# Attention and quantised feed-forward on one core: the softmax weights turned by VectorE and DMAs over DRAM, one place later

## The chip, the cores and the metric

One core of a Trainium2 chip runs the whole program. The metric is device time in microseconds (us): the median of the runs, 797.94 us before the change. TensorE does matrix products and turns matrices, VectorE and ScalarE work elementwise and on rows, GpSimd (POOL in the profile) takes elementwise work that needs no PSUM, and SyncE (SP) issues the DMAs.

## The reference

16 sequences of 256 tokens, 256 features. Attention has 16 query heads and 4 key/value heads of 128; a query sees itself and the 31 tokens before it (the window), and the first 4 tokens (the sink). The feed-forward part is a product with rows and weights rounded to 8 bits.

```python
# x: (16, 256, 256); layernorm without gain
x = x + attn(layernorm(x))
x = x + ffn(layernorm(x))

# attn: q = x @ wq.T (16 heads of 128), k, v = x @ wk.T, x @ wv.T (4 heads, each shared by 4 query heads)
mask = (k <= q) & ((k < 4) | (k >= q - 31))
scores = q . k / sqrt(128)
ex = exp(where(mask, scores, lowest) - rowmax) * mask
out = (ex / max(sum(ex), 1e-9)) @ v ;  return out @ wo.T

# ffn: per row of x and of weight: scale = max|.| / 127, rounded to int8
y = (x_q @ w_q.T) * x_scale * w_scale + bias
```

## The kernel before

**Tiles.** Activations are kept transposed. A *unit* (n, g, t) is one sequence, one key/value head g with its 4 query heads, and one half t of the tokens; 16 x 4 x 2 = 128 units. A unit has four blocks of 32 queries; with 4 heads these are 128 rows, which meet only 68 keys: the 4 sink keys, the 32 of the block before, and their own 32. So the scores of a unit are four products of 128x128 by 128x68 (`pss`, L503). A float32 product is two passes on TensorE, a transpose one.

**One unit's way.** VectorE scales and masks the scores out of PSUM (L514) and takes the row maximum (L516); ScalarE takes four exponentials with their sums (L523); VectorE divides (L530 to L533). Then the weights, 128 queries x 68 keys, must have keys on the partitions: TensorE turns each block (`ptd`, L508), and ScalarE copies the result to SBUF (`ad`, L511). With the values `vw`, laid out as 68 rows per block, four products give `po` (L539), which ScalarE copies to `oT` (L551). The output weights give `py` (L578, L594).

**The order** is written out by hand, one iteration i per unit, and each engine keeps it (`in_written_order`, L21). In iteration i TensorE runs: the scores of unit i with the transposes of unit i-1 between them (L496 to L508); a part of `py` for an earlier unit; `po` of unit i-1; a *chunk* in some iterations, that is the seven products for the keys or values of two heads of the next sequence (L444, L454); then the seven products for two query heads (`pq`, L470) that are used later. Keys, values, queries and most of `py` use a seven-product (Strassen-Winograd) scheme; the sums that put its results together (`combine`, L281 to L297) run on VectorE for the queries, at the start of the next iteration after L516, and on GpSimd for the chunks. The sums on the attention output before `py` (`left_sums`, L246 to L249) run on GpSimd.

For a fast output, part 0 of `py` (12 passes) comes in iteration i+2 and part 1 (16 passes) in i+3, where unit i is the second half of a head. So even iterations have 16 passes, and odd ones have 12 passes and a chunk: chunks stand in slots -5 (values of heads 0, 1), -3 (keys 0, 1), -1 (keys 2, 3) and +1 (values 2, 3), counted from the first unit of their sequence (L738).

**PSUM banks around the chunk.** The queries have two banks, q0 and q1. A chunk takes one bank of the pool `ps_m` and one of these two, the one that holds the first four results of the `pq` before it (`banks_of_chunk`, L276). The combine operations L293 and L294 read that bank; L295 to L297 read the other.

**Keys and values.** When GpSimd has combined a key chunk into `ktmp`, the keys are copied into 68 columns per block (`keys_to`, L382): two large copies by VectorE (L387, L388), two of 64 columns by ScalarE (L389, L390). This happens 1 iteration after the chunk for heads 0, 1 and 2 after it for heads 2, 3 (`keys_late`). Values go from SBUF to SBUF by 11 DMAs per pair of heads (`values_to`, L392).

**The rest of VectorE's work** stands at the ends of certain iterations: the combine of `py` and the addition to x (L602), the statistics, the norm (`norm`, L624 to L627, with L182), the rounding (L630) and the output (L654) of the feed-forward part in consecutive iterations from slot `done`+1 on (L768), and the norm of a later sequence (L182).

Of the kernel before, what the change touches and what calls it, by code (L numbers as in the profile page):

```python
# [34 lines left out]
def kernel(  # L35
# [27 lines left out]
    SB = T // QB  # L63
    NK = SINK + 2 * QB
    assert WIN == QB and HG * QB == P
    SCALE = 1.0 / math.sqrt(D)
# [4 lines left out]
    p2 = ctx.enter_context(tc.tile_pool(name="p2", bufs=2))  # L71
    p3 = ctx.enter_context(tc.tile_pool(name="p3", bufs=3))
    ps_s = ctx.enter_context(tc.tile_pool(name="ps_s", bufs=1, space=bass.MemoryType.PSUM))
    ps_t = ctx.enter_context(tc.tile_pool(name="ps_t", bufs=1, space=bass.MemoryType.PSUM))
# [28 lines left out]
    wo_sb = const.tile([P, H, DM], FP, name="wo_sb")  # L103
    wf_sb = p1.tile([P, NC, DM], FP, name="wf_sb")
    bias_bc = const.tile([P, DM], FP, name="bias_bc")
# [28 lines left out]
    def keep(ap, base, cm, step):  # L134
# [4 lines left out]
        )  # L139

    def mask_steps():


        def build(b):
            pool.memset(masks[:, 0, b, :], 0.0)
            if b < 2:
                pool.memset(masks[:, 0, b, 0:SINK], NEG)
            if b == 0:
                pool.memset(masks[:, 0, b, SINK : SINK + QB], NEG)
            for h in range(HG):  # L150
                m = masks[h * QB : (h + 1) * QB, 0, b, :]
                keep(m[:, SINK:], QB, 1, -1)
                if b == 1:
                    keep(m[:, 2 * SINK :], SINK - 1, -1, 1)
                elif b == 2:
                    keep(m[:, SINK:], -1, -1, 1)

        def others():
            like = masks[:, 0, 2:3, :]
            pool.tensor_copy(masks[:, 0, 3:, :], like)  # L160
            pool.tensor_copy(masks[:, 1], like.to_broadcast([P, NBLK, NK]))
            pool.tensor_copy(ident16, ident)
            pool.memset(ones, 1.0)

        return [lambda b=b: build(b) for b in (2, 0, 1)] + [others]
# [22 lines left out]
    def ffn_weight_steps():  # L188
        ws = p1.tile([P, NC], FP, name="ws")
        wq16 = p1.tile([P, NC, DM], BF, name="wq16")  # L190
        diag = p1.tile([P, NC, P], FP, name="diag")

# [189 lines left out]
    def keys_to(n, g, kb):  # L382

        k = p2.tile([P, 2, SB, NK], FP, tag="kt", name=f"kt_{n}_{g}")
        for e in range(2):
            kt[n, g + e] = k[:, e]
        dve.tensor_copy(k[:, :, :, SINK + QB :], kb)  # L387
        dve.tensor_copy(k[:, :, 1:, SINK : SINK + QB], kb[:, :, 0 : SB - 1, :])  # L388
        act.copy(k[:, :, 0, SINK : SINK + QB], kb[:, :, 0, :])  # L389
        act.copy(k[:, :, :, 0:SINK], kb[:, :, 0, 0:SINK].unsqueeze(2).to_broadcast([P, 2, SB, SINK]))  # L390

    def values_to(w, v, tiles):  # L392

        if 0 in tiles:
            sp.dma_start(w[0:SINK], v[0:SINK, 0].unsqueeze(1).to_broadcast([SINK, SB, 2 * D]))
            sp.dma_start(w[SINK : SINK + QB, 0, :], v[0:QB, 0])
            sp.dma_start(w[SINK : SINK + QB, NBLK, :], v[P - QB : P, 0])
        for t in tiles:
            sp.dma_start(w[SINK + QB : NK, t * NBLK, :], v[0:QB, t])
            for k in range(1, NBLK):  # L400
                sp.dma_start(w[SINK:NK, t * NBLK + k, :], v[(k - 1) * QB : (k + 1) * QB, t])

# [10 lines left out]
    def plain_values(n, t):  # L413
        pv = ps_m.tile([P, G * D], FP, tag="m", name=f"pv_{n}_{t}")
        for c in range(NC):
            pe.matmul(  # L416
                pv, xnT[n][:, c, t * P : (t + 1) * P], wv_sb[:, c, :],
                start=(c == 0), stop=(c == NC - 1),
            )

        def rest():
            v = p2.tile([P, 3, 2, D], FP, tag="vt", name=f"vt_{n}_{t}")
            act.copy(v[:, 0:2].rearrange("p j e d -> p (j e d)"), pv)
            for p in range(2):
                if t == 0:
                    vw[n, p] = p3.tile([NK, SB, 2 * D], FP, tag="vw", name=f"vw_{n}_{p}")
                plain_values_to(vw[n, p], v[:, p].rearrange("p e d -> p (e d)"), t)

        return rest

    def plain_values_to(w, v, t):
        if t == 0:
            sp.dma_start(w[0:SINK], v[0:SINK].unsqueeze(1).to_broadcast([SINK, SB, 2 * D]))
            sp.dma_start(w[SINK : SINK + QB, 0, :], v[0:QB])
            sp.dma_start(w[SINK : SINK + QB, NBLK, :], v[P - QB : P])
        sp.dma_start(w[SINK + QB : NK, t * NBLK, :], v[0:QB])
        for k in range(1, NBLK):
            sp.dma_start(w[SINK:NK, t * NBLK + k, :], v[(k - 1) * QB : (k + 1) * QB])

# [11 lines left out]
    def values(n, pair):  # L451
        p = banks_of_chunk(f"pv_{n}_{pair}")
        for to, left, right in products(p, factors(n, wv_sb, wv_sums, pair), SMALL_FIRST):
            pe.matmul(to, right, left, start=True, stop=True)  # L454
        v = p2.tile([P, 3, 2, D], FP, tag="vt", name=f"vt_{n}_{pair}")
        w = vw[n, pair] = p3.tile([NK, SB, 2 * D], FP, tag="vw", name=f"vw_{n}_{pair}")
        return Products(p, f"v_{n}_{pair}", (v[:, 0:3:2, 0], v[:, 2, 1], v[:, 1, 0], v[:, 0:2, 1])), (
            lambda: values_to(w, v.rearrange("p j e d -> p j (e d)"), range(NT))
        )

# [31 lines left out]
    def scores_and_turned(u, w):  # L492
# [5 lines left out]
        if w:  # L498
            sw = ss.pop(w)
            ptd = ps_t.tile([NK, NBLK * P], FP, tag="t", name=f"ptd_{w[0]}_{w[1]}_{w[2]}")  # L500
        for k in range(NBLK):
# [5 lines left out]
            if w:  # L507
                pe.transpose(ptd[:, k * P : (k + 1) * P], sw[:, k, :], ident)  # L508
        if w:
            ad = ads[w] = p2.tile([NK, NBLK * P], FP, tag="ad", name=f"ad_{w[0]}_{w[1]}_{w[2]}")  # L510
            act.copy(ad, ptd)  # L511
        if u:
            s = ss[u] = p3.tile([P, NBLK, NK], FP, tag="sc", name=f"s_{n}_{g}_{t}")
            dve.scalar_tensor_tensor(s, pss, SCALE, masks[:, t], ALU.mult, ALU.add)  # L514
            nmax = p3.tile([P, NBLK], FP, tag="nmax", name=f"nmax_{n}_{g}_{t}")
            dve.tensor_reduce(nmax, s, AX.X, ALU.max, negate=True)  # L516
        return nmax if u else None

    def exponentials(n, g, t, nmax):
        s = ss[n, g, t]  # L520
        sm = p3.tile([P, NBLK], FP, tag="sm", name=f"sm_{n}_{g}_{t}")
        for k in range(NBLK):
            act.activation(  # L523
                s[:, k, :], s[:, k, :], AF.Exp, bias=nmax[:, k : k + 1], scale=1.0,
                accum_out=sm[:, k : k + 1],
# [3 lines left out]
    def normalised(n, g, t, sm):  # L529
        dve.tensor_tensor(sm, sm, floor, ALU.max)  # L530
        dve.reciprocal(sm, sm)
        s = ss[n, g, t]
        dve.tensor_mul(s, s, sm.unsqueeze(2).to_broadcast([P, NBLK, NK]))  # L533

    def times_values(n, g, t):
        ad = ads.pop((n, g, t))
        po = ps_m.tile([P, NBLK, HG, QB], FP, tag="m", name=f"po_{n}_{g}_{t}")
        for k in range(NBLK):
            pe.matmul(  # L539
                po[:, k].rearrange("p h i -> p (h i)"), vw[n, g // 2][:, t * NBLK + k, g % 2 * D : (g % 2 + 1) * D],  # L540
                ad[:, k * P : (k + 1) * P], start=True, stop=True,
            )
# [172 lines left out]


    units = [(n, g, t) for n in range(B) for g in range(G) for t in range(NT)]
    units[-3], units[-2] = units[-2], units[-3]
    PER = G * NT

    LAST = ((3, 3), (4, 5), (5, 5), (6, 6), (6, 7), (7, 7), (8, 8), (9, 9))

# [5 lines left out]
    for n in range(B):  # L728
# [8 lines left out]
        else:  # L737
            for slot, f, pair in ((-5, values, 0), (-3, keys, 0), (-1, keys, 1), (1, values, 1)):  # L738
                at(n * PER + slot, lambda f=f, n=n, pair=pair: f(n, pair), chunks)
# [8 lines left out]
    for i, (n, g, t) in enumerate(units):  # L748
        if n == 0:
            at(i + 3, lambda u=(n, g, t): projected(*u), shares)  # L750
        elif n == B - 1:
# [3 lines left out]
        elif t == 1:  # L755
            for part in range(2):
                at(i + 2 + part, lambda u=(n, g, part): projected_fast(*u), shares)
    at(0, lambda: weight_sums(wv_sb, wv_sums))
# [8 lines left out]
    for n in range(B - 1):  # L767
        done = (n + 1) * PER + 2  # L768
        for k, slot in enumerate((1, 2, 3, 4, 5)):
# [24 lines left out]

    waiting, later = None, {}
    for i in range(len(units) + 2):
        u, w = get(i), get(i - 1)
        chunk = chunks.pop(i, [None])[0]
        nmax = scores_and_turned(u, w)
        if waiting:  # L800
            waiting.first()
# [12 lines left out]
        if not shared or i >= (B - 1) * PER:  # L814
            rests += [queries(n, h) for n, h in asked.get(i, []) if not fast_queries(n, h)]
            asked[i] = [u for u in asked.get(i, []) if fast_queries(*u)]
        values_out = times_values(*w) if w else None
        if chunk:
# [4 lines left out]
        if u:  # L823
            normalised(*u, sm)
        if w:
            values_out()
        for f in later.pop(i, []):
# [7 lines left out]
        if chunk:  # L835
# [3 lines left out]
            else:  # L839
                chunk_rest()  # L840
        for f in combined:
# [45 lines left out]
```

## Time and profile before

| what | us |
|---|---|
| median of three runs | 797.94 (797.91 to 798.2) |
| the profiled execution: its own time | 797.91 |
| its span in the profile | 796.1 |
| granted TensorE clock over the span | 0.997 |
| one steady sequence, 8 units (400.47 to 448.82) | 48.35 |
| of it busy: TensorE / VectorE / ScalarE / GpSimd | 48.35 / 37.17 / 26.84 / 32.30 |
| DMA engines busy in that stretch | 0.15 |

A group line of the profile names the line, the engine, the operation, output<-input, the shape and the count; then busy us and mean ns of one; then the idle time of the engine just before, with what ended it. A matmul's record runs until its results are in PSUM and overlaps its neighbours, so the pace of TensorE is read from starts, not from durations. PEld is the load of the stationary operand, which runs ahead under other products. In the timeline the columns are start, time, engine, line, and how many records are merged. TensorE is busy 50.00 of every 50 us until 775 us; the tail from there to 796 is the last feed-forward part.

### The profile page before, as it was taken

How to read it: one execution, taken by the hardware profiler on the slowest of the kernel's cores; microseconds unless marked ns; L12 is line 12 of the kernel's file. 1: busy time of each engine (PE TensorE's matmuls, PEld its weight loads, DVE VectorE, ACT ScalarE, POOL GpSimd, SP SyncE). 2: the span in 40 equal slices, each digit the busy share in tenths (PEclk: the TensorE clock that was granted, in tenths of full speed). 3: DMA queues.
4: the chain of work that ended last, by engine and by line, in shares of the span. 5: the costliest groups of instructions: out<-in, count | busy, mean ns of one | idle time of the engine just before them, and what ended most of it. 6: DMA issues, size and time to landing. Idle time of an engine off the chain costs nothing.

```text
span 796.1 us, 19508 instructions
## 1 busy us (share of the span) xinstructions
PE 787.0 (99%) x7019; PEld 776.2 (97%) x7019; DVE 588.7 (74%) x1716; ACT 433.4 (54%) x1617; POOL 514.3 (65%) x813
## 2 busy tenths in 40 slices
PE   9999999999999999999999999999999999999996
PEld 7999999999999999999999999999999999999994
DVE  3577787787777877877877877877778778778675
ACT  3655555555555555555555555555555555555552
POOL 4768866676676675676666766766766756766423
PEclk9999999999999999999999999999999999999998
DMA  6510201111020110201202011110202102011001
GB/s 217 164 29 14 58 21 48 31 36 49 23 60 17 54 40 15 71 21 42 37 23 63 21 48 31 36 49 22 60 18 56 36 14 71 21 30 36 22 22 33
DMA packets 43808, 35.09 MB, mean 44 GB/s; under 512 B 14144, under 2 KB 42176, under 8 KB 43712
## 3 DMA queue, kind: packets, MB, share of 16 engines
q1 hardware_dynamic: 43712, 33.84, 16.6%
q8 instruction: 56, 0.92, 0.5%
q14 instruction: 40, 0.33, 0.1%
HBM read 9.83 MB, written 4.19 MB: 18 GB/s over the span
## 4 chain that ended last, share of the span: by engine, by line
PE 99%; DVE 1%; issue 0%; POOL 0%; ACT 0%; DVEq 0%; POOLq 0%
PE pq L470 23%; PE py L594 22%; PE po L539 14%; PE pss L503 11%; PE ptd L508 7%; PE pk L444 6%; PE pv L454 6%; PE py L578 3%; PE pq L481 2%; PE pa L649 1%; PE xt L361 1%; PE warm L779 0%; PE pv L416 0%; PE pk L407 0%; PE xt L379 0%; DVE y_last L706 0%
## 5 line engine op out<-in xcount | busy, mean ns | idle before, releaser
L511 ACT COPY ad<-ptd 68x512 f32<-68x512 f32 x128 | 74.4, 581 | 227.8 <-PE ptd L508 227.8
L523 ACT ACTIVATE s<-s,nmax 128x68 f32<-128x68 f32 x512 | 173.6, 340 | 17.4 <-DVE nmax L516 11.0
L503 PE MATMUL pss<-kt,qt 128*128 128x68 f32 x1024 | 151.6, 250 | 0.0
L503 PEld LDWEIGHTS pss<-kt,qt 128*128 128x128 f32 x1024 | 147.4, 191 | 0.7 <-issue 0.5
L508 PE MATMUL ptd<-ident,s 128*68 128x128 f32 x512 | 139.1, 273 | 0.0
L539 PE MATMUL po<-ad,vw 68*128 68x128 f32 x1024 | 135.3, 275 | 0.0
L514 DVE SCALAR_TENSOR_TENSOR s<-pss,masks 128x272 f32<-128x272 f32 x128 | 56.3, 440 | 96.7 <-PE pss L503 92.7
L539 PEld LDWEIGHTS po<-ad,vw 68*128 68x128 f32 x1024 | 125.8, 192 | 1.0 <-ACT ad L511 0.3
L470 PE MATMUL pq<-xs,wq_sums 128*128 128x128 f32 x714 | 118.6, 275 | 0.0
L470 PEld LDWEIGHTS pq<-xs,wq_sums 128*128 128x128 f32 x714 | 98.8, 192 | 0.0
L523 ACT ACTIVATION_READ_ACCUMULATOR s<-s,nmax 128x1 f32 x512 | 95.6, 187 | 0.0
L551 ACT COPY oT<-po 128x512 f32<-128x512 f32 x129 | 75.4, 585 | 30.0 <-PE po L539 30.0
L508 PEld LDWEIGHTS ptd<-ident,s 128*68 128x68 f32 x512 | 84.7, 165 | 0.1
L594 PE MATMUL py<-wo_sums,os 128*128 128x128 f32 x672 | 84.2, 275 | 0.0
L594 PEld LDWEIGHTS py<-wo_sums,os 128*128 128x128 f32 x672 | 79.4, 192 | 0.0
L293 POOL TENSOR_TENSOR ktmp<-b_k 128x256 f32<-128x256 f32 x30 | 21.9, 728 | 86.1 <-ACT b_k L314 86.1
L293 POOL TENSOR_TENSOR vt<-b_v 128x256 f32<-128x256 f32 x30 | 21.8, 728 | 81.2 <-ACT b_v L314 81.2
L246 POOL TENSOR_TENSOR os<-oT 128x256 f32<-128x256 f32 x56 | 46.8, 836 | 40.7 <-ACT oT L551 39.5
L470 PE MATMUL pq<-xnT,wq_sb 128*128 128x128 f32 x476 | 72.6, 275 | 0.0
L470 PEld LDWEIGHTS pq<-xnT,wq_sb 128*128 128x128 f32 x476 | 62.7, 192 | 0.0
L533 DVE TENSOR_TENSOR s<-s,sm 128x272 f32<-128x272 f32 x128 | 58.9, 460 | 4.4
L594 PE MATMUL py<-wo_sb,oT 128*128 128x128 f32 x448 | 59.2, 275 | 0.0
(181 smaller groups left out, 1824.8 us busy)
## 6 DMA issues: line engine op xcount, KB each, us to landing
vw<-vt SPq DMA_DIRECT2D x192, 64.0 KB
vw<-vt SPq DMA_DIRECT2D x160, 32.0 KB
x<-in_x_dram SPq DMA_DIRECT2D x15, 256.0 KB
out_dram<-y SPq DMA_DIRECT2D x15, 256.0 KB
wq_sb<-in_wqT_dram SPq DMA_DIRECT2D x4, 512.0 KB
wo_sb<-in_woT_dram SPq DMA_DIRECT2D x4, 512.0 KB
wv_sb<-in_wvT_dram SPq DMA_DIRECT2D x1, 512.0 KB
wk_sb<-in_wkT_dram SPq DMA_DIRECT2D x1, 512.0 KB
```

The lines of the kernel that those rows point to most:

```text
L444: pe.matmul(to, left, right, start=True, stop=True)
L454: pe.matmul(to, right, left, start=True, stop=True)
L470: pe.matmul(to, left, right, start=True, stop=True)
L503: pe.matmul(pss[:, k, :], qt[n, g][:, t, k].rearrange("p h i -> p (h i)"), kt[n, g][:, t * NBLK + k, :], start=True, stop=True,)
L508: pe.transpose(ptd[:, k * P : (k + 1) * P], sw[:, k, :], ident)
L511: act.copy(ad, ptd)
L514: dve.scalar_tensor_tensor(s, pss, SCALE, masks[:, t], ALU.mult, ALU.add)
L523: act.activation(s[:, k, :], s[:, k, :], AF.Exp, bias=nmax[:, k : k + 1], scale=1.0, accum_out=sm[:, k : k + 1],)
L533: dve.tensor_mul(s, s, sm.unsqueeze(2).to_broadcast([P, NBLK, NK]))
L539: pe.matmul(po[:, k].rearrange("p h i -> p (h i)"), vw[n, g // 2][:, t * NBLK + k, g % 2 * D : (g % 2 + 1) * D], ad[:, k * P : (k + 1) * P ...
L551: act.copy(o[:, t, hs].rearrange("p h (k i) -> p k h i", i=QB), po[:, :, hs])
L594: pe.matmul(region(py, i), left[:, e], right[:, e], start=(g == 0 and e == 0 and i in (1, 4)), stop=(g == G - 1 and e == 1 and i in (7, 3)),)
```

## The change

Units 4 to 122 no longer have their weights turned by TensorE (`lag` 2). VectorE divides in place, in one of two score buffers of 96 columns per block whose last 28 are cleared once, and turns it in 32x32 blocks into `z`. SP stores `z` to DRAM (`zd`), and, in the next iteration, after that has landed, loads it back as `ad`, with 96 rows of keys: row 3j+c is key j of chunk c (0 the block before, 1 its own, 2 the sink). `po` of such a unit comes two iterations after its scores instead of one. The first four and the last five units keep TensorE's transpose, now of 96 columns.

With that the parts of `py` move one iteration later and the chunks to slots -4, -2, 0 and +2 (for sequence 1: -1, -3, 0, +2), so that chunks stand in even iterations, still beside 12 passes. The feed-forward steps move one iteration later. All four key copies are ScalarE's now. Values go to DRAM in one store and come back to three standing buffers by three loads (four the first time each buffer is used), issued one iteration after the chunk.

```diff
+    scores = [const.tile([P, NBLK, NKP], FP, name=f"scores_{j}") for j in range(2)]
+    for j in range(2):
+        pool.memset(scores[j], 0.0)
...
-        dve.tensor_copy(k[:, :, :, SINK + QB :], kb)
-        dve.tensor_copy(k[:, :, 1:, SINK : SINK + QB], kb[:, :, 0 : SB - 1, :])
-        act.copy(k[:, :, 0, SINK : SINK + QB], kb[:, :, 0, :])
-        act.copy(k[:, :, :, 0:SINK], kb[:, :, 0, 0:SINK].unsqueeze(2).to_broadcast([P, 2, SB, SINK]))
+        act.copy(k[:, :, :, QB : 2 * QB], kb)
+        act.copy(k[:, :, 1:, 0:QB], kb[:, :, 0 : SB - 1, :])
+        act.copy(k[:, :, 0, 0:QB], kb[:, :, 0, :])
+        act.copy(k[:, :, :, 2 * QB :], kb[:, :, 0, 0:SINK].unsqueeze(2).to_broadcast([P, 2, SB, SINK]))
...
+    def values_to(n, pair, v, tiles=range(NT)):
+        w, fresh = vw[n, pair], 2 * n + pair < 3
+        b0, b1 = tiles[0] * NBLK, (tiles[-1] + 1) * NBLK
+        sp.dma_start(w[1:NKP:NCH, b0:b1], v[b0:b1].rearrange("b k d -> k b d"))
+        c1 = min(b1 + 1, SB)
+        sp.dma_start(w[0:NKP:NCH, b0 + 1 : c1], v[b0 : c1 - 1].rearrange("b k d -> k b d"))
+        if b0 == 0:
+            rows = QB if fresh else SINK
+            sp.dma_start(w[2 : NCH * (rows - 1) + 3 : NCH], v[0, 0:rows].unsqueeze(1).to_broadcast([rows, SB, 2 * D]))
...
+    def weights_turned(n, g, t):
+        s = ss.pop((n, g, t))
+        z = p2.tile([P, NCH, NBLK, QB], FP, tag="z", name=f"z_{n}_{g}_{t}")
+        dve.transpose(z, s.rearrange("p k (c i) -> p c k i", c=NCH))
+        zd = dram.tile([P, NCH * P], FP, tag="zd", name=f"zd_{n}_{g}_{t}")
+        sp.dma_start(zd, z.rearrange("p c k i -> p (c k i)"))
+        def back():
+            ad = ads[n, g, t] = p3.tile([NKP, HG, NBLK, QB], FP, tag="ad", name=f"ad_{n}_{g}_{t}")
+            sp.dma_start(
+                ad.rearrange("p h k i -> p h (k i)"), zd.rearrange("(h j) (c x) -> (j c) h x", h=HG, c=NCH)
+            )
+        return back
...
-            for slot, f, pair in ((-5, values, 0), (-3, keys, 0), (-1, keys, 1), (1, values, 1)):
+            for slot, f, pair in zip((-4, -2, 0, 2) if n > 1 else (-1, -3, 0, 2), (values, keys, keys, values), (0, 0, 1, 1)):
...
+    FIRST, TAIL = 4, len(units) - 5
+    def lag(i):
+        return 2 if FIRST <= i < TAIL else 1
...
-                at(i + 2 + part, lambda u=(n, g, part): projected_fast(*u), shares)
+                at(i + 3 + part, lambda u=(n, g, part): projected_fast(*u), shares)
...
-        done = (n + 1) * PER + 2
+        done = (n + 1) * PER + 3
...
-        u, w = get(i), get(i - 1)
+        u, w = get(i), get(i - 1) if lag(i - 1) == 1 else None
...
+        if i - 1 in ways:
+            ways.pop(i - 1)()
...
-        values_out = times_values(*w) if w else None
+        values_out = [times_values(*units[j]) for j in (i - 2, i - 1) if get(j) and j + lag(j) == i]
...
         if u:
             normalised(*u, sm)
+            if lag(i) == 2:
+                ways[i] = weights_turned(*u)
```

## The prediction

> **What bounds the kernel.** I read the page's busy and chain lines first, then the two rows that the change is about.
>
> ```profile
> PE 787.0 (99%) x7019; PEld 776.2 (97%) x7019; DVE 588.7 (74%) x1716; ACT 433.4 (54%) x1617; POOL 514.3 (65%) x813
> ...
> PE 99%; DVE 1%; issue 0%; POOL 0%; ACT 0%; DVEq 0%; POOLq 0%
> PE pq L470 23%; PE py L594 22%; PE po L539 14%; PE pss L503 11%; PE ptd L508 7%; PE pk L444 6%; PE pv L454 6%; PE py L578 3%; PE pq L481 2%; PE pa L649 1%; PE xt L361 1%; PE warm L779 0%; PE pv L416 0%; PE pk L407 0%; PE xt L379 0%; DVE y_last L706 0%
> ...
> L503 PE MATMUL pss<-kt,qt 128*128 128x68 f32 x1024 | 151.6, 250 | 0.0
> ...
> L508 PE MATMUL ptd<-ident,s 128*68 128x128 f32 x512 | 139.1, 273 | 0.0
> ```
>
> TensorE is the chain from end to end, so only its own pace and new waits of it count. The transposes (L508) look like 139 us of busy time, or 7% of the chain (56 us). Neither is what removing them gives. The timeline of TensorE shows the scores alone (unit 0, which has nothing to turn) and with transposes between (unit 68):
>
> ```profile
> 14.91 1.00 PE L503 MATMUL pss<-kt,qt 128*128 128x68 f32 x8
> 15.75 0.43 PE L481 MATMUL pq<-xnT,wq_sb 128*128 128x256 f32 x1
> ```
> ```profile
> 424.63 0.34 PE L503 MATMUL pss<-kt,qt 128*128 128x68 f32 x2
> 424.80 0.27 PE L508 MATMUL ptd<-ident,s 128*68 128x128 f32 x1
> 424.91 0.34 PE L503 MATMUL pss<-kt,qt 128*128 128x68 f32 x2
> ...
> 425.65 0.27 PE L508 MATMUL ptd<-ident,s 128*68 128x128 f32 x1
> 425.76 1.50 PE L594 MATMUL py<-wo_sums,os 128*128 128x128 f32 x12
> ```
>
> With transposes a unit takes 425.76 - 424.63 = 1.13 us. Alone, single passes start 112 ns apart (14.968, 15.080, ... 15.638), though 68 columns stream in 59 ns (14.909 to 14.968): each pass waits for its 128-column weight load. Eight are 8 x 0.112 = 0.89 us. **A unit loses 0.24 us, not 0.45**: a transpose was partly run under weight loads. [...]
>
> **The change, part by part.** Times after S, the start of an iteration's scores, come from this trace; r is the iteration modulo 8.
>
> 1. Units 4 to 122 lose TensorE's transpose: 119 x 0.24 = **-28.6**. Eight of the nine others, where scores are interleaved too, load 96 columns instead of 68, bounded by the step from 60 to 112 ns in proportion: 8 x 4 x 0.02 = +0.7.
>
> 2. ScalarE loses 119 copies `ad` (0.58 us each) and gets the two large key copies of VectorE (L387, L388). Most of the first is worth nothing (L511 idles 227.8 us on TensorE). But the first keys of a sequence move from slot -3 to -2, and their copies run at the end of iteration r=7, right before the scores that read them. That iteration is 0.89 + 1.78 (16 passes of py) + 0.89 (po) + 1.56 (pq) = 5.13. ScalarE's copy of po starts 0.20 after po ends:
>
> ```profile
> 411.45 0.59 ACT L551 COPY oT<-po 128x512 f32<-128x512 f32 x1
> 411.93 0.26 ACT L389 COPY kt<-ktmp 128x64 f32<-128x64 f32 x1
> 412.07 0.26 ACT L390 COPY kt<-ktmp 128x64 f32<-128x64 f32 x1
> ```
>
> So: 3.57 + 0.20 = 3.77; oT 0.48 to the next start; a 512 copy 0.48, a 448 copy 0.43 (in proportion), 0.14, 0.26: ready at 5.56. Semaphore and weight load take 0.22 more (below): 5.78 - 5.13 = 0.65, in sequences 2 to 15: **+9.1**. The copies' source is SBUF, whose row is 64 wide only (253 ns): between 0.3 (half the pace) and 0.9.
>
> 3. VectorE gets a 128x384 block transpose per unit. No row has one. Bounds by the nearest rows: a 512-wide copy (L387) 0.42 us; a 256-wide tensor_scalar under contention (L182, xn) 0.82, in proportion 1.23. I take the line through L294 (128 wide, 291 ns) and L293 (256, 424): 0.56 us, of which 0.48 until the next start, since it moves its elements like these. It also waits for the product before it (0.115 more than the usual 0.36). So VectorE's iteration grows by T = 0.59 (bounds 0.45 and 1.3). [...]
>
> VectorE has time for this on average (37.2 of 48.35 us per sequence), but not in two places. The chunk products (L444, L454) write a bank which the second combine operation (L294) must have read. The trace already shows this as a wait, 25 ns:
>
> ```profile
> 428.84 0.44 DVE L533 TENSOR_TENSOR s<-s,sm 128x272 f32<-128x272 f32 x1
> 429.20 1.14 DVE L182 TENSOR_SCALAR h<-x,mv_f 128x256 f32<-128x256 f32 x2
> ...
> 431.62 0.43 DVE L514 SCALAR_TENSOR_TENSOR s<-pss,masks 128x272 f32<-128x272 f32 x1
> ...
> 432.88 0.29 DVE L294 TENSOR_TENSOR qt<-pq,qt 128x128 f32<-128x128 f32 x1
> ```
> ```profile
> 433.37 0.41 PE L444 MATMUL pk<-xs,wk_sb 128*128 128x128 f32 x2
> 433.62 0.39 PE L444 MATMUL pk<-xs,wk_sums 128*128 128x128 f32 x2
> ```
>
> L294 ends at 433.17, 1.55 after L514 starts; the chunk can run 0.22 later (semaphore, weight load). So a chunk waits if L514 starts later than X, with X + 1.77 = the chunk's place. That place was 1.13 + 1.34 + 0.89 = 3.36; without transposes 3.12, so X may be 1.35. In the changed order L514 starts at 1.04 when unhindered, and VectorE is free 3.35 + T later. Chunks now stand in even iterations, after odd ones of 5.13:
> - r=6: the FFN norm (429.20 to 431.62 = 2.42) is in r=5. X = 1.04 + 3.35 + T + 2.42 - 5.13 = 1.68 + T. Wait 0.33 + T = 0.92, 14 times: **+12.9**.
> - r=4: the output's combine (417.56 to 419.36 = 1.80) is in r=3. X = 1.06 + T; wait T - 0.29 = 0.30, 13 times: **+3.9**.
>
> Behind the waiting chunk stand pq and the next scores: all later work shifts, nothing makes it up.
>
> 4. The weights' way by DRAM. By the trace's semaphore events a 256 KB store (L656) lands 2.16 us after its issue, a 256 KB load (L88) 2.9, a 64 KB copy 1.9 to 2.0. Write plus read: 5.1 us. SP also has to pass what is queued between: for r=2 a values store that waits for GpSimd and a load of x. The chunk ends at 4.69, GpSimd 3.88 later (410.77 to 414.65 in this trace): 8.57, or 2.32 in the next iteration, whose scores start 6.25 later. Two issues of about 0.5 stand ahead, so the read is issued at 3.45 and lands at 6.4 to 6.8 with the load ahead of it; po, two iterations on, needs it at 5.13 + 0.89 + 1.34 = 7.36. r=0 (an output store ahead) has 0.9 us left, odd units over 2. So 0; bounds 0 and 0.6 x 14 = 8. DMA engines are 15% busy in these stages.
>
> 5. Values: 11 DMAs of SP (about 0.6 us each) become one store and three loads, two iterations or more before use. First sequence: the store lands by 14.5 behind the weights, the rows by 19 to 20; po starts at 23.98; if that cover were gone, each us late would be a us. GpSimd clears two score buffers between 1.4 and 3.6, when it has nothing else. All 0.
>
> 6. Tail: the FFN of sequence 14 ends one slot later, its pa and two VectorE operations (0.86) now stand between the last po and the last output; half is hidden: +0.5. The wider product in the last units: +0.2.
>
> **Sum**: -28.6 - 0.4 (old 25 ns waits) + 0.7 + 9.1 + 12.9 + 3.9 + 0.7 = -1.7. In T it is -17.6 + 27 T, even at T = 0.65. From the profiled execution's own 797.91 (span 796.1; median of the runs 797.94): **796.2**.
>
> **Rivals.**
> - The saving is kept. If neither wait comes (bank free earlier, keys copied earlier), 797.9 - 28.6 - 0.4 + 1.4 = 770; if only the key wait is missing 787; if only the chunk waits are, 779. For it: VectorE and ScalarE have average room. Against: the 25 ns wait stands in the trace, and the order of the copies is written.
> - Slower: the block transpose is dear. At 1.0 us (T = 1.0) the chunk waits are 0.71 and 1.33: 807; at the upper row 815. It decides from T = 0.65. For it: L182 and L627 run at two to three times their usual time beside GpSimd. Against: the tensor_tensor rows do not.
> - Slower: weights land late. If write and read take 6.5 instead of 5.1, po waits about 0.8 in r=2 and 0.5 in r=0, 14 times: 796 + 18 = 814; it decides from 5.8. Against: the measured landings.
> - It does less than it says: nine units keep the old way, which is in the sum.
>
> **Chances.** Forecast (both waits, T 0.45 to 0.75: 792 to 801) 0.5; saving kept in full or half 0.2; transpose dear 0.2; late weights 0.1. 0.2% (1.6 us) is about what a measurement of this kernel can tell from no change. Of the forecast's 0.5, 0.2 lies below 796.3, 0.2 within and 0.1 above 799.5. Faster: 0.2 + 0.2 = 0.4. Same: 0.2. Slower: 0.1 + 0.2 + 0.1 = 0.4. The forecast's own range is 792 to 801; the range for 8 in 10 reaches to the half-kept saving and to T = 1: 784 to 808.
>
> **What would show it.** Right: scores' passes 112 ns apart; TensorE idle before the key chunk on L305 (14 x about 0.9) and before the first scores of a sequence on ScalarE's key copies (14 x 0.65); block transpose near 0.56 us; po not waiting on DMA. Wrong: TensorE still 99% busy at 770; po waiting for `ad`; a transpose over 0.8 us; a wait that I have not named, such as py on VectorE in r=4 or on GpSimd.

## The result and the profile after

The changed kernel takes **796.38 us** (795.30 to 796.91, nine runs) against 798.00 (797.65 to 798.32, nine runs): a ratio of 0.9977, 95% interval 0.9967 to 0.9987. So the change gains 0.2%. The forecast was 796.2. The profiled execution took 796.78, its span is 795.0; the lines, table and waits below are those of the profiled executions.

The page of the changed kernel: busy time, the chain by engine and line, then two rows of groups.

```profile
PE 768.1 (97%) x6543; PEld 750.7 (94%) x6543; DVE 614.8 (77%) x1771; ACT 399.8 (50%) x1562; POOL 512.7 (64%) x815
...
PE 77%; DVE 16%; ACT 4%; DMA 1%; issue 1%; POOL 0%; DVEq 0%; ACTq 0%; POOLq 0%
...
L526 PE MATMUL pss<-kt,qt 128*128 128x68 f32 x1024 | 131.9, 269 | 5.4 <-ACT kt L401 5.4
...
L548 DVE STREAM_TRANSPOSE z<-scores 128x384 f32<-128x384 f32 x119 | 68.8, 578 | 4.1
```

TensorE lost 19 us of busy time and its span only one: it was 99% busy and is 97%. The chain no longer runs on TensorE from end to end; a fifth of it goes through VectorE and ScalarE. Where TensorE waits for them is the next view, TensorE's waits (us in total, times, longest).

```profile
PE pk L463 <- DVE qt L305: 8.5, 14, 0.6
PE pss L526 <- ACT kt L401: 5.4, 14, 0.4
...
PE pv L473 <- DVE qt L305: 0.8, 1, 0.8
...
PE po L589 <- DMA ad<-zd: 0.7, 2, 0.5
```

The first two are the waits of the forecast, 14 times each, on the instructions that it named: L305, and ScalarE's key copies, of which L401 is the last. A wait is shown shorter than its cost, because a matmul's record reaches 0.16 us and more into the gap: the starts give the cost. TensorE's timeline in one sequence (unit 70 is r=6, unit 71 is r=7):

```profile
434.10 1.06 PE L589 MATMUL po<-ad,vw 96*128 96x128 f32 x8
435.76 0.46 PE L463 MATMUL pk<-xs,wk_sb 128*128 128x128 f32 x2 [0.60 <-DVE qt L305]
...
443.87 0.39 PE L493 MATMUL pq<-xnT,wq_sums 128*128 128x128 f32 x2
444.64 1.11 PE L526 MATMUL pss<-kt,qt 128*128 128x68 f32 x8 [0.38 <-ACT kt L401]
```

Elsewhere the same eight passes of `po` are followed after 0.89 us; here the chunk starts 1.66 later, a gap of 0.77. The sum is best read from the time between the starts of two units' scores. Medians over units 16 to 119, by r, in us, for ten kernels of this study (the experiments below say what each is):

| kernel | r=0 | 1 | 2 | 3 | 4 | 5 | 6 | 7 | median of the runs |
|---|---|---|---|---|---|---|---|---|---|
| before | 5.37 | 6.93 | 5.37 | 6.49 | 5.37 | 6.52 | 5.37 | 6.93 | 798.00 |
| after | 6.79 | 5.57 | 6.25 | 5.14 | 6.37 | 5.14 | 7.10 | 5.68 | 796.38 |
| keys first | 6.69 | 5.57 | 6.25 | 5.14 | 6.37 | 5.14 | 7.09 | 5.14 | 788.21 |
| combine first | 6.79 | 5.57 | 6.25 | 5.14 | 6.25 | 5.14 | 6.48 | 5.68 | 785.81 |
| turned twice | 6.79 | 5.57 | 6.25 | 5.14 | 6.98 | 5.14 | 10.00 | 5.68 | 837.14 |
| before, no turn | 5.14 | 7.06 | 5.14 | 6.25 | 5.14 | 6.46 | 5.14 | 6.69 | 775.97 |
| no block turn | 6.79 | 5.57 | 6.25 | 5.14 | 6.25 | 5.14 | 6.49 | 5.68 | 788.12 |
| keys on VectorE | 7.31 | 5.57 | 6.25 | 5.14 | 6.37 | 5.14 | 7.09 | 5.95 | 807.88 |
| first three edits | 6.95 | 5.57 | 6.25 | 5.14 | 6.25 | 5.14 | 7.54 | 5.14 | 798.55 |
| last three edits | 6.79 | 5.57 | 6.25 | 5.14 | 6.25 | 5.14 | 6.48 | 5.16 | 779.74 |

An iteration without a chunk went from 5.37 to 5.14, one with a chunk from 6.49 to 6.25: this is the transposes' 0.24. What lies above 5.14 and 6.25 in the line "after" (and above 6.69 in r=0 and 5.57 in r=1, which also hold `pa` and `xt`) are the waits.

### The profile page after: what moved, and what is told of

Same layout as the page of the kernel before. It is cut to its first block, busy times and chain, and to the rows that moved or that the text cites. A ratio compares the mean times of both kernels' runs of the same rounds, so it can differ in the third digit from the quotient of the medians.

```text
span 795.0 us, 18758 instructions
## 1 busy us (share of the span) xinstructions
PE 768.1 (97%) x6543; PEld 750.7 (94%) x6543; DVE 614.8 (77%) x1771; ACT 399.8 (50%) x1562; POOL 512.7 (64%) x815
## 4 chain that ended last, share of the span: by engine, by line
PE 77%; DVE 16%; ACT 4%; DMA 1%; issue 1%; POOL 0%; DVEq 0%; ACTq 0%; POOLq 0%
PE pq L493 18%; PE py L644 17%; PE pss L526 12%; PE po L589 11%; PE pk L463 6%; PE pv L473 6%; PE py L628 3%; DVE h L193 2%; DVE nmax L539 2%; DVE scores L537 2%; PE pq L504 2%; DVE xs L676 1%; DVE qt L304 1%; DMA ad<-zd 1%; ACT oT L601 1%
## 5 line engine op out<-in xcount | busy, mean ns | idle before, releaser
L564 ACT ACTIVATE scores<-scores,nmax 128x68 f32<-128x68 f32 x512 | 173.5, 340 | 276.9 <-DVE nmax L539 276.9
L589 PE MATMUL po<-ad,vw 96*128 96x128 f32 x1024 | 135.5, 275 | 1.1 <-DMA ad<-zd 0.7
L526 PEld LDWEIGHTS pss<-kt,qt 128*128 128x128 f32 x1024 | 126.3, 192 | 8.8 <-ACT kt L401 8.0
L589 PEld LDWEIGHTS po<-ad,vw 96*128 96x128 f32 x1024 | 125.7, 192 | 2.5 <-issue 1.8
L537 DVE SCALAR_TENSOR_TENSOR scores<-pss,masks 128x272 f32<-128x272 f32 x128 | 56.1, 438 | 90.3 <-PE pss L526 89.8
L564 ACT ACTIVATION_READ_ACCUMULATOR scores<-scores,nmax 128x1 f32 x512 | 95.7, 187 | 0.0
L548 DVE STREAM_TRANSPOSE z<-scores 128x384 f32<-128x384 f32 x119 | 68.8, 578 | 4.1
L539 DVE TENSOR_REDUCE nmax<-scores 128x4 f32<-128x272 f32 x128 | 55.8, 436 | 4.4
L583 DVE TENSOR_TENSOR scores<-scores,sm 128x272 f32<-128x272 f32 x119 | 54.4, 457 | 4.1
L644 PEld LDWEIGHTS py<-wo_sb,oT 128*128 128x128 f32 x448 | 54.5, 192 | 0.0
```

What stands on the lines that cost most here:

```text
L526: pe.matmul(pss[:, k, :], qt[n, g][:, t, k].rearrange("p h i -> p (h i)"), kt[n, g][:, t * NBLK + k, :], start=True, stop=True,)
L537: dve.scalar_tensor_tensor(s[:, :, 0:NK], pss, SCALE, masks[:, t], ALU.mult, ALU.add)
L539: dve.tensor_reduce(nmax, s[:, :, 0:NK], AX.X, ALU.max, negate=True)
L548: dve.transpose(z, s.rearrange("p k (c i) -> p c k i", c=NCH))
L564: act.activation(s[:, k, 0:NK], s[:, k, 0:NK], AF.Exp, bias=nmax[:, k : k + 1], scale=1.0, accum_out=sm[:, k : k + 1],)
L589: pe.matmul(po[:, k], vw[n, g // 2][:, t * NBLK + k, g % 2 * D : (g % 2 + 1) * D], ad[:, :, k], start=True, stop=True,)
```

## The experiments

**Theory**: TensorE's passes are 28 us shorter, and two late engines take nearly all of it back at three places, before the chunks of r=6 and r=4 (VectorE's L305) and before the first scores of a sequence (ScalarE's key copies). **Rivals**: the gain of the removal is smaller than its passes; VectorE's load costs time in every unit; the way over DRAM is what is late.

**1. The removal alone, in the kernel before.** `some` is a constant tile.

```diff
-                pe.transpose(ptd[:, k * P : (k + 1) * P], sw[:, k, :], ident)
...
-            act.copy(ad, ptd)
+            act.copy(ad, some)
```

> The kernel before, with nothing moved, without TensorE's transposes of the weights: ScalarE copies a constant tile into ad instead, so the product with the values takes a constant for the softmax weights and does not wait for them. This prices the removal alone. Theory (a transpose is worth 0.24 us per unit, and the earlier chunk in r=5 then waits 0.27 instead of 0.03 for L294): 797.9 - 128 x 0.24 + 14 x 0.24 = 771. Rival 1 (a transpose is worth its record, 139 us in all, or its share of the chain, 56): 660 or 742. Rival 2 (the removal is no gain by itself, as TensorE then waits for other engines in the old order): over 780.

775.97 us (0.9723 of before; 0.9709 to 0.9738). Iterations without a chunk take 5.14 and the others 6.25, as in the changed kernel, so 0.24 per unit is the price, and not the 139 us of the records or the 56 of the chain. Above that, r=5 waits 0.21 for VectorE (0.27 expected) and r=1 0.37, which was not expected: 14 x 0.58 = 8 of the 128 x 0.24 = 31 are lost even here. So the rest of the change, with everything that replaces the transposes, costs 20 us.

**2. The wait for the keys.** The first run changes the slot, the second the engine.

```diff
-            for slot, f, pair in zip((-4, -2, 0, 2) if n > 1 else (-1, -3, 0, 2), (values, keys, keys, values), (0, 0, 1, 1)):
+            for slot, f, pair in zip((-4, -2, 0, 2) if n > 1 else (-1, -3, 0, 2), (values, keys, keys, values) if n == 1 else (keys, values, keys, values), (0, 0, 1, 1)):
```

> The changed kernel with the chunks in slots -4 and -2 exchanged from the second sequence on: keys of heads 0 and 1 first, then values. The key copies then run in iteration r=5 instead of r=7. Theory (the first scores of a sequence wait because ScalarE copies the keys behind oT in the iteration right before): the wait of 0.547 us and the longer second pass behind it (0.05) go in 14 sequences, some 8 to 9 us: 796.4 - 8.5 = 788, and r=7 takes 5.14 us instead of 5.68. Rival 1 (something else is late at the same place, such as GpSimd's sums or the values, which now start two iterations later): the wait stays or comes back at po, 795 to 797. Rival 2 (the copies in r=5 push oT and with it the next chunk): r=6 grows by what r=7 loses.

```diff
-        act.copy(k[:, :, :, QB : 2 * QB], kb)
-        act.copy(k[:, :, 1:, 0:QB], kb[:, :, 0 : SB - 1, :])
+        dve.tensor_copy(k[:, :, :, QB : 2 * QB], kb)
+        dve.tensor_copy(k[:, :, 1:, 0:QB], kb[:, :, 0 : SB - 1, :])
```

> The changed kernel with the two large key copies (L398, L399) on VectorE, where the kernel before had them, and all else as changed. Theory (the wait for the keys comes from the slot: the copies run in the iteration right before the first scores, on whichever engine): VectorE's chain in r=7 is over 4.98 us after the scores begin, the copies take it to 5.82, the wait is 0.9 instead of 0.55: 796.4 + 14 x 0.36 = 801, from 797 to 803. Rival (the engine is the cause: ScalarE is late, VectorE would have been in time): the wait goes, 787.

Keys first: 788.21 us, as the theory had it; r=7 is 5.14 and r=0 6.69, so the wait cost 0.54 + 0.10 = 0.64 per sequence. Keys on VectorE: 807.88, slower still. The rival falls: the slot makes the wait. Only 801 was expected, since a second wait was missed: the scores' later blocks read L399's result, and wait once more for it. r=7 and r=0 together are 0.79 longer than after, 14 x 0.79 = 11. TensorE's waits in that run:

```profile
PE pss L526 <- DVE kt L398: 9.1, 14, 0.7
...
PE pss L526 <- DVE kt L399: 4.6, 14, 0.3
```

**3. The wait of the chunks.** First VectorE's order, then its load, less and more of it.

```diff
+        ahead = 2 if chunk and waiting and i % PER in (4, 6) else 0
+        if ahead:
+            waiting.first()
+            waiting.combine(dve, range(ahead))
         nmax = scores_and_turned(u, w)
...
-            waiting.combine(dve)
+            waiting.combine(dve, range(ahead, 5))
```

> The changed kernel with the first two operations of the queries' combine (L304, L305) ahead of the scaling and the maximum of the scores (L537, L539) on VectorE, only in the iterations r=4 and r=6, where a chunk waits for L305. Theory (the chunk waits for its bank, and the bank for VectorE's order): L305 ends 0.9 us earlier, the gap before the chunk falls from 0.88 to 0.11 in r=6 and from 0.15 to 0.11 in r=4; r=6 takes 6.25 instead of 7.09, r=4 6.25 instead of 6.36: 13 to 14 us less, 783. Rival 1 (VectorE is simply too late there in all its work; the 0.7 us by which scores come later turns up as a wait of the next scores, of po or of the next chunk): 790 to 800. Rival 2 (the chunk waits for another thing that ends at the same time): no change, 796.

```diff
-        z = p2.tile([P, NCH, NBLK, QB], FP, tag="z", name=f"z_{n}_{g}_{t}")
-        dve.transpose(z, s.rearrange("p k (c i) -> p c k i", c=NCH))
+        z = some
```

> The changed kernel without the block transposes (L548): SP stores a constant tile instead of z, all DMAs and waits of po stay, and the product with the values takes constants for the softmax weights. This prices VectorE's part alone. Theory (0.61 us of VectorE per unit cost time only before the chunks of r=6 and r=4): the gap of r=6 falls from 0.84 to 0.23, that of r=4 goes: 14 x 0.61 + 1.5 = 10 us less, 786. Rival 1 (the chunks wait because the odd iteration before them is short and carries the norm, whatever the transposes): within 2 us of 796. Rival 2 (it costs in each unit): 796.4 - 119 x 0.5 = 737.

```diff
-        dve.transpose(z, s.rearrange("p k (c i) -> p c k i", c=NCH))
+        for _ in range(2):
+            dve.transpose(z, s.rearrange("p k (c i) -> p c k i", c=NCH))
```

> The changed kernel with each block transpose (L548) issued twice into the same z, 119 more of 0.5 us on VectorE. Theory (VectorE's time costs only where a chunk waits for L305, r=6 and r=4): each of these gaps grows by 0.5: 14 x 0.5 + 13 x 0.5 = 13.5 us, 810; the other iterations keep their lengths, except r=2, whose weights now land 0.5 us later, up to 0.5 x 14 = 7 more: 810 to 817. Rival 1 (every VectorE microsecond counts): 119 x 0.5 = 60, 856. Rival 2 (the chunk's wait is not VectorE's): 796 to 798.

Combine first: 785.81 us, r=4 at 6.25 and r=6 at 6.48. The chunk starts on time. The 0.23 left is lost in `pq`: the exponentials now come 0.65 later, and ScalarE copies the chunk's banks, one of which `pq` needs, only behind them. Here that is read from the order alone; in experiment 5 the same wait is long enough to be listed. No block turn: 788.12 us (786 expected), the scaling of r=6 starts 1.59 us after the scores instead of 2.19, so T is 0.60 there. Both rivals fall with it: rival 1 had at most 2 us less, and for rival 2 (each unit pays) the other six iterations would be shorter than in the changed kernel, which they are not.

Turned twice: **837.14, where the theory had at most 817**. The starts of r=6 show two things that it did not have. The gap before the chunk grew by 1.28 us, not 0.5, and behind it TensorE is slow (four passes: 0.45 us elsewhere):

```profile
353.34 1.06 PE L590 MATMUL po<-ad,vw 96*128 96x128 f32 x8
356.27 0.46 PE L463 MATMUL pk<-xs,wk_sb 128*128 128x128 f32 x2 [1.88 <-DVE qt L305]
356.57 0.39 PE L463 MATMUL pk<-xs,wk_sums 128*128 128x128 f32 x2
...
357.90 1.06 PE L463 MATMUL pk<-xs,wk_sums 128*128 128x128 f32 x4
358.76 1.06 PE L493 MATMUL pq<-xnT,wq_sb 128*128 128x128 f32 x4
...
360.43 0.39 PE L493 MATMUL pq<-xs,wq_sb 128*128 128x128 f32 x2
```

From 357.1 to 360.4 passes start 213 ns apart instead of 112, some 1.6 us lost per time; 11 of the 14 sequences have it. The granted clock is 0.50 in that stretch and 1.00 in the 3.4 us on both sides of it; over the run it is 0.974, against 0.997. To see what sets off which, the extra work was put on the units of r=5 alone.

```diff
         dve.transpose(z, s.rearrange("p k (c i) -> p c k i", c=NCH))
+        if units.index((n, g, t)) % PER == 5:
+            dve.transpose(z, s.rearrange("p k (c i) -> p c k i", c=NCH))
```

> The changed kernel with the whole block transpose issued twice, only for the units of r=5: 14 of the 119. When all units had it, the run took 837.1. Theory (only r=5's counts for r=6, and the slow passes there follow from the gap): r=6 takes 9.6 to 10.0 as it did then, r=4 stays at 6.37: 796.4 + 14 x 2.5 = 831. Rival 1 (VectorE's whole load counted): 796.4 + 40.7 x 14/119 = 801. Rival 2 (the slow passes came from the load of all units and not from the gap): 796.4 + 14 x 1.3 = 815.

```diff
+        if units.index((n, g, t)) % PER == 5:
+            dve.transpose(z[:, 0], s[:, :, 0:QB])
```

> The changed kernel with one more block transpose of a third of z (128x128), only for the units of r=5. The gap before the chunk of r=6 grows from 0.77 to 1.1 or, should the small operations behind it grow as well, 1.5. Theory (VectorE's microsecond in r=5 is a microsecond before the chunk, nothing else changes): 796.4 + 14 x 0.3 = 800.6, up to 807. Rival (a gap over about a microsecond already slows TensorE's passes from 112 to 213 ns behind it, as the gap of 2.04 did when all units had two transposes): 1.2 us more each, 817 to 824.

833.46 and 832.60 us. The 14 units of r=5 alone give all that is slow in r=6 (12 of 14 with slow passes): the theory of the first of these two expectations holds, and the load of all units does not count for r=6. But a third of a transpose costs as much as a whole one, and the same gap, 2.05 us. Here are VectorE and GpSimd in r=5 of the run with a third:

```profile
347.22 0.58 DVE L548 STREAM_TRANSPOSE z<-scores 128x384 f32<-128x384 f32 x1
347.84 0.31 DVE L550 STREAM_TRANSPOSE z<-scores 128x128 f32<-128x128 f32 x1
348.07 1.59 DVE L193 TENSOR_SCALAR h<-x,mv_f 128x256 f32<-128x256 f32 x2
349.69 0.69 DVE L678 TENSOR_REDUCE xs<-h 128x2 f32<-128x512 f32 x1
350.41 1.08 DVE L679 TENSOR_SCALAR xs<-xs 128x2 f32<-128x2 f32 x1
351.41 0.43 DVE L537 SCALAR_TENSOR_TENSOR scores<-pss,masks 128x272 f32<-128x272 f32 x1
```
```profile
349.47 0.77 POOL L260 TENSOR_TENSOR os<-oT,os 128x256 f32<-128x256 f32 x1
350.21 1.26 POOL L680 TENSOR_TENSOR x<-x,bias_bc 128x512 f32<-128x512 f32 x1
```

L679 handles two elements per row and takes 1.08 us. It ends at 351.49, GpSimd's addition at 351.47. In the changed kernel the same operation (L677 there) ends with GpSimd's operation before that one (434.15 and 434.11) and takes 0.54; a little more work ahead of it, and it meets the next, longer one. So I moved the addition away.

```diff
             dve.tensor_scalar(xs, xs, 1.0 / 127.0, 1e-12, ALU.mult, ALU.max)
-            pool.tensor_add(xt, xt, bias_bc.unsqueeze(1).to_broadcast([P, NT, DM]))
...
             pool.tensor_scalar(h16, h, MAGIC, None, ALU.subtract)
+            pool.tensor_add(xt, xt, bias_bc.unsqueeze(1).to_broadcast([P, NT, DM]))
```

> The kernel of the last but one run (one more block transpose of a third of z in r=5) with GpSimd's 128x512 addition of the bias moved out of r=5 to the end of the rounding step in r=6. There the third of a transpose moved VectorE by 1.28 us, since L679 (2 elements) took 1.08 instead of 0.54: it ended when GpSimd's addition did (351.47). Theory (VectorE's tensor_scalar from SBUF stands still until the GpSimd instruction beside it ends, so that delays come in steps of GpSimd's instructions): without that instruction L679 is short, the gap before the chunk of r=6 is 0.8 to 1.5 instead of 2.05; without the slow passes that is 796 to 807, with them (should a gap of that size set them off too) 815 to 825. Rival (L679 is slow for another reason): gap 2.05 and 832 as before.

801.22 us. VectorE in r=5 again:

```profile
339.39 0.69 DVE L678 TENSOR_REDUCE xs<-h 128x2 f32<-128x512 f32 x1
340.11 0.17 DVE L679 TENSOR_SCALAR xs<-xs 128x2 f32<-128x2 f32 x1
340.19 0.43 DVE L537 SCALAR_TENSOR_TENSOR scores<-pss,masks 128x272 f32<-128x272 f32 x1
```

The two elements take 0.17; GpSimd's last operation ended at 339.94. The gap is 1.13 us, and no pass in r=6 is slow. Both guesses hold here, and they are separate: beside GpSimd's addition L679 ended 0.02 us after it and the gap was 2.05, without it 1.13; and slow passes followed most gaps of 2.05 and none of 1.13.

The records of the granted clock also tell the 35 sequences with slow passes from the 7 without, in the three runs with gaps of 2.05. Each slow stretch lasts 3.413 us in them, and within a run they start whole multiples of 3.413 us apart (15 times that most often). Laid on a grid of that step, the 35 gaps have 2.02 to 2.05 us within one step, and the step after it is the slow one; the 7 others lie across a boundary, with at most 1.90 us on either side.

**4. The weights' way over DRAM.** In the changed kernel `po` waits for `ad` in r=2 of four sequences (units 18, 42, 66, 90), by the starts 0.31, 0.53, 0.47 and 0.76 us. These are three sequences apart. The DMA view of the stretch 117 to 123 us, around unit 18:

```profile
q1 hardware_dynamic: 816, 0.66, 34.7%
q8 instruction: 1, 0.02, 1.5%
issues: line engine op xcount, KB each, median us to landing
ad<-zd SPq DMA_DIRECT2D x2, 192.0 KB
out_dram<-y SPq DMA_DIRECT2D x1, 256.0 KB
```

A packet of 16 KB of the queue that the view names instruction (a code packet, for short) takes 1.45 us, from 1.25 after the load is issued; 1.5% of 16 engines over 6 us is one engine for that time. Such a packet stands in each of the four stretches, and the load lands 4.3 to 4.7 us after its issue. In nine stretches from unit 26 on there is none, the load lands after 2.6 to 2.8, and `po` does not wait. A fifth packet stands in that of unit 114: there the load lands after 3.8, still in time for `po`.

```diff
-            sp.dma_start(out_v[n], y)
+        def store():
+            sp.dma_start(out_v[n], y)
...
-        return [stats, norm, quantise, turn, linear]
+        return [stats, norm, quantise, turn, linear, store]
...
-        for k, slot in enumerate((1, 2, 3, 4, 5)):
+        for k, slot in enumerate((1, 2, 3, 4, 5, 6)):
```

> The changed kernel with the store of the output (L706) issued one iteration later, so that on SP it no longer stands ahead of the load of ad in r=1. In the changed kernel that load is issued 3.64 us after the scores of r=1 begin and lands 2.7 later, but 4.3 to 4.7 later in the four sequences (units 18, 42, 66, 90) where a 16 KB instruction packet of 0.9 to 1.4 us falls on it; po then waits 0.3 to 0.8. Theory (the margin is used up by the queue ahead, the packet only shows it): the load is issued some 2 us earlier, all r=2 take 6.25, 2.1 us less: 794.3. Rival (the late pieces come from the DMAs' own contention, whatever the issue): waits of po stay in three or four sequences, 796.4.

795.38 us, 1.0 less, though the runs of the two kernels overlap (794.82 to 795.71 here, 795.30 to 796.91 there); from unit 18 on all r=2 take 6.25. One wait of 0.99 in r=4 (unit 92) is new, where a code packet again stands in the stretch and the load of `ad` behind that of x. The order on SP sets the margin. That the packet does the rest is what all these cases share, no more than that, as no run could take a packet away; and it does not always do so, as in this run the load for unit 116 lands after 2.7 with a packet in its stretch.

**5. Together.** The first try took the three edits above, with all five combine operations ahead in r=6, to be rid of the wait of `pq`.

> The changed kernel with three edits: the chunks of slots -4 and -2 exchanged (keys first); the queries' combine ahead of the scores' scaling on VectorE, two operations in r=4 and all five in r=6, since with two alone pq waited there 0.2 for the other bank; the output store one iteration later. Theory (the three waits are separate places and add up): 788.2 and 785.8 each took 8.2 and 10.6 from 796.4; r=6 at 6.25 takes 3.2 more, the store 2.1: 796.4 - 8.2 - 10.6 - 3.2 - 2.1 = 772.3. Rival 1 (taking one wait away makes the next one later in the same sequence, such as VectorE in r=7 or the values that now start later): 776 to 786. Rival 2: the later exponentials of r=6 delay its weights' way so that po waits in r=0: over 780.

798.55 us: the expected gain of 24 is gone, and neither rival had that. TensorE's waits say where to:

```profile
PE pq L493 <- ACT b_v L325: 13.8, 14, 1.0
PE pa L699 <- DMA hT<-h: 6.1, 7, 1.3
```

With the combine first the exponentials of r=6 come 1.71 us later, ScalarE copies the chunk's banks only behind them, and `pq` needs one of these banks: r=6 is 7.54. And the values, now in r=6, put their loads ahead of `hT` on SP in r=7, so `pa` waits in half of the sequences. Neither queue was in the theory. The second try keeps the changed kernel's order of chunks, so that the values' loads stay where they were. It takes two operations ahead in r=4 and r=6, the later store, and, for the keys, their copies (in `later`) ahead of that to `oT` (in `values_out`) on ScalarE:

```diff
+        for f in later.pop(i, []):
+            f()
         for f in values_out:
             f()
-        for f in later.pop(i, []):
-            f()
```

> The changed kernel with its own order of chunks and three edits: two operations of the combine ahead of the scores' scaling in r=4 and r=6; the key copies ahead of oT on ScalarE; the output store one iteration later. GpSimd has ktmp ready 2.6 us into r=7 and ScalarE is through with the exponentials at 3.5, so the copies can end at 4.9, before the next scores at 5.14, and the DMAs of r=7 stay as they are. Theory: the savings of the three places add up, 796.4 - 10.6 - 9 - 1 = 776, with r=7 at 5.14 and r=0 at 6.69. Rival 1 (oT of r=7 now comes 1.4 us later, its sums on GpSimd too, and py waits in r=0): 780 to 790. Rival 2 (as with the three edits before, one gain undoes another through a queue that is not yet seen): over 786.

**779.74 us**, 0.9770 of before (0.9757 to 0.9784), the best of the kernels here that compute the whole. The expectation was 3.7 too low. By the table units 16 to 119 gain (0.52 + 0.62 + 0.12) x 13 and the 2.1 of r=2, 18.4, and the profiled execution (778.73 against 796.78) has 18.0 of it; by the medians of the runs the gain is 16.6, and no trace shows where the other 1.4 went. Two shortfalls are seen: r=0 stays at 6.79 and not at 6.69, as the keys still end 0.02 after the scores could start, and the edges of the program gained nothing. The wait of `pq` in r=6, 0.23 x 14 = 3.2, is what the next edit would go for.

## Why the prediction was right, and where it was not

- **Passes** (-28.6): 0.23 and 0.24 per unit by the iteration lengths, and by experiment 1.
- **Transposes of 96 columns** (+0.7): 0. A unit with them takes 1.13 us, like one with 68, though the record of a load went from 166 to 178 ns (medians). The step in proportion to the columns was the author's estimate, and the starts do not show it.
- **Key wait** (+9.1): 0.64 x 14 = 9.0. The slot as the cause and the engine hold (experiment 2), but that the sizes meet so well is partly luck. The copies end 5.63 after the scores start (5.56 worked out) and the first pass follows 0.05 later (0.22 taken), which makes 0.54; the other 0.10 is lost in r=0, behind that pass, and was not in the sum.
- **Chunk in r=6** (+12.9): 7.10 - 6.25 = 0.85, x 14 = 11.8. VectorE's scaling starts 2.19 after the scores, 2.27 was worked out. **In r=4** (+3.9): 0.12 x 13 = 1.5; the start is 1.46, not 1.65. The block transpose takes 0.578 us (0.56 taken) and T is 0.60 (0.59), so the excess lies in the rest of the two sums: without transposes the starts are 1.59 and 1.14 (experiment 3), against 1.68 and 1.06 with T at 0. In r=4 the two do not add: VectorE's extra 0.60 moves the start by 0.32 alone.
- **Way over DRAM** (0, bounds 0 to 8): 2.1 by the starts in four sequences of the profiled execution. The tight unit was r=0's, whose load stands behind the output store, not r=2's; and the measured landings, all of undisturbed transfers, left out the code packets.
- **Start and tail** (+0.7): outside units 16 to 119 the kernel is 0.9 us longer, where the steps of the forecast make it 0.7 shorter. What was missed is at the change of lag: a wait of 1.2 in unit 4 for `z` of unit 3, and one of 1.0 for L305 in unit 7.

So the mechanisms and their places were right, and the 0.2 us between forecast and result are luck: 3.5 us too much on the chunks against 1.6 at the edges and 2.1 on the DMAs too little.

**One step of it was wrong and did not show**: the sum as a straight line in T, "-17.6 + 27 T", and with it the price of the rival "the block transpose is dear" (807 at T = 1.0). Below T = 0.6 it is flatter, since r=4 stops waiting (788 without the transpose, where the line gives 780). Above, with each transpose doubled (T near 1.1), the line gives 810 and the run took 837: a little more on VectorE in r=5 is 36 us at once, by GpSimd's instruction and then by the slow passes. With a third of a transpose more in r=5 alone the run was at 833. The reason given for that rival holds for the small operation (L627 takes 0.61 beside GpSimd in the kernel before, and 0.17 alone in experiment 3, which is more than two to three times), not for the block transpose itself (577 to 580 ns in the changed kernel). The range 784 to 808 was too narrow above for that rival.

## What to carry to other kernels

Price a removed TensorE instruction by the spacing of the passes' starts around it, and then look at once for what was just in time before: the shorter iteration makes every other engine late at its tightest place, and here that took 27 of 28 us. A wait on one engine's order is bought back by that order, but each reordering has to be followed through every queue that it passes: taking away the same three waits gave 17 us or none, by where the DMAs and bank copies then stood. A margin on a busy engine should be measured by experiment with a little more work, as the cost need not be a line.

## What the runs showed of the hardware

- **A small VectorE operation ended when GpSimd's instruction did.** The operation on 2 elements per row (L679, L677 in the changed kernel) took 0.17 us alone, and 0.54 or 1.08 beside GpSimd, each time to within 0.03 us of the end of GpSimd's instruction, in all 14 sequences of each run (experiment 3: with the addition moved; the changed kernel; with a third of a transpose). The block transpose took 577 to 580 ns in all of its 119 executions in the changed kernel.
- **A gap on TensorE can cost more than itself.** After gaps of 2.05 us passes ran at 213 ns instead of 112, at a granted clock of 0.50, for 3.0 to 3.4 us in 35 of 42 cases (three runs), and in none after gaps of 1.13 (14) or 0.77 (14), nor after those of up to 1.45 in "first three edits". On the grid of 3.413 us on which a run's slow stretches start, the 35 gaps had 2.02 us or more within one step and the 7 others at most 1.90, which parts all 42 cases.
- **A load landed later in most stretches with a code packet**: the queue named instruction moved 52 packets of 16 KB, of 0.9 to 1.7 us each, in one execution. A load of 192 KB, which lands in 16 parts, took up to 2 us more (4.7 instead of 2.7) where one stood in its stretch.
